# Routed tiles' tokens turned by transposing transfers instead of TensorE transposes

## The chip, the core and the metric

The kernel runs on one core of a Trainium2 chip. A core has TensorE (PE in the profile; its weight loads are PEld), VectorE (DVE), ScalarE (ACT), GpSimd (POOL) and SyncE (SP). They run their own instruction streams and wait for each other by semaphores. Sixteen DMA engines move data; in this kernel nearly all transfers are issued by SP, one after the other. The metric is the device time in microseconds (us) from start to end.

## What is computed

A decoder layer over 8 sequences of 256 tokens with 256 features each: causal self-attention with 16 heads, a cross attention with three gated recurrent updates, and a mixture-of-experts feed-forward part. Each of the three ends with a residual and a layer norm. All is float32. The change lies in the last part, of which the reference is, shortened:

```python
def _L0_ffn_ref(x, gate_w, gate_b, sh_w1, sh_b1, sh_w2, sh_b2, ew1, eb1, ew2, eb2):
    router_probs = softmax(einsum('bsd,de->bse', x, gate_w) + gate_b)
    expert_values, expert_indices = top_k(router_probs, k=2)
    expert_values = expert_values / (sum(expert_values, axis=-1, keepdims=True) + 1e-09)
    h = gelu(einsum('bsd,edi->bsei', x, ew1) + eb1)
    all_outputs = einsum('bsei,eid->bsed', h, ew2) + eb2
    moe_out = einsum('bse,bsed->bsd', weights_E, all_outputs)
    return x + _mlp(x, sh_w1, sh_b1, sh_w2, sh_b2) + moe_out
```

There are 8 experts, each an MLP 256 -> 1024 -> 256, of which each token uses its best two, and one shared MLP for every token.

## The kernel before

The 2048 tokens stand in four blocks of 512. Attention comes first (to about 340 us), then the recurrent part with the routing of finished blocks woven in (to about 640 us), then the experts.

**Routing by tables in DRAM.** For each token and each of its two experts the kernel computes a row number in a table `xd` in DRAM, in which each expert owns a stretch of rows, and GpSimd scatters the tokens there (`place`, L914). The tables `tei` and `tri` then tell, for every tile of work, which expert it belongs to and at which row it starts. A pair tile has 256 rows, a single tile 128. There are 21 tiles that always run, in the order pair, pair, single, five times, and then six pairs. Two more single tiles (`RARE`) stand under a condition and run only if a table says so.

**One tile.** Its parts, with the lines of the profile:

- `tile_fetch` (L1143, L1145): SP loads the row number from `tri` into a register and issues the transfer of the tokens, `xg`, tokens on partitions; 256 KB for a pair.
- `tile_weights` (L1157 to L1163): SP loads the expert's number from `tei` and issues the transfer of the first weight `w1` (1 MB; L1162) and its bias `bt`.
- `tile_turn` (L1178, L1180): TensorE transposes `xg` in blocks of 128x128 into PSUM, and VectorE copies the result to `xgT`, features on partitions.
- `tile_up` (L1075, L1084): `up`, in 16 float32 matmuls, each of which appears as two records in the profile, and the gelu on ScalarE.
- `tile_weights2` (L1169, L1170): transfer of the second weight `w2` (1 MB) and its bias `b2t`.
- `tile_down` (L1089, L618, L1193): the matmuls of the second layer, VectorE adds the bias into `yo`, and SP stores it into the table `yd`.

**Order.** For TensorE and ScalarE the order is that of the program text. For VectorE, GpSimd and SP a scheduler chooses the order in this stage, so it need not be that of the text; it moves register loads from `tei` and `tri` far ahead. In the text, step k of the loop over tiles is: up of k, fetch of k+3, first weight of k+2, turn of k+1, down of k-1, second weight of k+1. Both weights have two buffers: the w1 of tile k+2 waits for the up of tile k, the w2 of k+1 for the down of k-1. `xg` has four buffers, `xgT` two.

**Around it.** Before the first tile, four of the eight units of the shared MLP run (`shared_up`, `shared_down`); the other four come after the last tile, together with the gathering of the experts' rows by GpSimd (`fetch_back`, L1203), their sum on VectorE (`take_back`), the last layer norm and the store of the result (`finish`).

**A transfer that transposes** is already in the attention stage: `split` (L388, and L391 for half of the words of the last block on GpSimd) copies the float32 words of a matrix of 128x768 into two planes of 16-bit halves, SP issues one transposing transfer of the 128x1536 words (L394), and `joined` (L400) has VectorE put the halves of the turned planes together.

Of the kernel before, what the change touches and what calls it, by code (L numbers as in the profile page):

```python
# [10 lines left out]
F32 = mybir.dt.float32  # L11
I32 = mybir.dt.int32
U16 = mybir.dt.uint16
# [4 lines left out]
B, S, D = 8, 256, 256  # L18
# [3 lines left out]
NE, FF = 8, 1024  # L22
P = 128
DC = D // P
# [13 lines left out]
RT = 256  # L38
# [7 lines left out]
TILES = [t for k in range(NOFTEN) for t in (2 * k, 2 * k + 1, NPAIRT + k)]  # L46
# [19 lines left out]
def decoder_kernel(  # L66
# [23 lines left out]
    nc = tc.nc  # L90
# [6 lines left out]
    def big(name):  # L97
        return pools["big"].tile([P, 2, 512], F32, tag="big", name=name)

    def bank(name):  # L100
        return pools["bk"].tile([P, 512], F32, tag="bk", name=name)
# [13 lines left out]
    XT = [act.tile([P, DC, BLK], F32, tag=f"XT{i}", name=f"XT{i}") for i in range(NBLK)]  # L115
# [5 lines left out]
    ident = const.tile([P, P], F32, name="ident")  # L121
# [46 lines left out]
    b1c = vec_sb[:, 0 : (NE + 1) * FC].rearrange("p (e c) -> p e c", c=FC)  # L168
# [36 lines left out]
    def load_shared():  # L205
        w1_sb = sh.tile([P, DC, FF], F32, name="sh1")
        w2_sb = sh.tile([P, FC, D], F32, name="sh2")
        nc.sync.dma_start(w1_sb, sh_w1.rearrange("(c p) f -> p c f", p=P))
        nc.sync.dma_start(w2_sb, sh_w2.rearrange("(c p) d -> p c d", p=P))
        return w1_sb, w2_sb  # L210
# [56 lines left out]
    with (  # L267
# [234 lines left out]
        for k in range(last + 1):  # L502
            i, j = divmod(k, 2 * NPAIR)
# [38 lines left out]
    shared = load_shared()  # L542
# [60 lines left out]
    for h in range(2):  # L603
        n = (NSINGLE + 1 - h) // 2
# [458 lines left out]
    f2 = ctx.enter_context(tc.tile_pool(name="f2", bufs=2))  # L1063
    f1 = ctx.enter_context(tc.tile_pool(name="f1", bufs=1))
    wff = ctx.enter_context(tc.tile_pool(name="wff", bufs=2))

    def up(w1_sb, bias, rhs, name):
        hT = fh.tile([P, FC, RT], F32, tag="hT", name=f"hT_{name}")
        w = rhs.shape[2]
        for c2 in range(FC // 2):  # L1070
            ph = big(f"ph_{name}_{c2}")
            for a in range(2):
                c = 2 * c2 + a
                for dc in range(DC):
                    nc.tensor.matmul(  # L1075
                        ph[:, a, 0:w],
                        w1_sb[:, dc, ts(c, P)],
                        rhs[:, dc, :],
                        start=dc == 0,
                        stop=dc == DC - 1,  # L1080
                    )
            for a in range(2):
                c = 2 * c2 + a
                nc.scalar.activation(hT[:, c, 0:w], ph[:, a, 0:w], AF.Gelu_apprx_tanh, bias=bias[:, c : c + 1])  # L1084
        return hT
# [15 lines left out]
    HT = {}  # L1101

    def shared_up(u):
        i, h = divmod(u, BLK // RT)
        HT["s", u] = up(shared[0], b1c[:, NE, :], XT[i][:, :, ts(h, RT)], f"s{u}")

    def shared_bias(u):

# [24 lines left out]
    TI = {}  # L1133

    def groups(t):
        return 2 if t < NPAIRT else 1
# [4 lines left out]
    def tile_fetch(t):  # L1141

        row = nc.sync.value_load(tri[0:1, t : t + 1], min_val=0, max_val=ROWS - RT)  # L1143
        xg = f2.tile([P, 2, D], F32, tag="xg", name=f"xg_{t}", bufs=4)[:, 0 : groups(t), :]
        load = nc.sync.dma_start(xg, rows_of(xd, row, t))  # L1145
        for put in puts:
            tc.add_manual_dep(
                load.ins,
                put.ins.name,
                mybir.DependencyInfo(mybir.DependencyClass.Sync, mybir.DependencyReason.DATA),  # L1150
                reason="rows of the table",
            )
        TI[t] = [row, xg]

    def tile_weights(t):

        e = nc.sync.value_load(tei[0:1, t : t + 1], min_val=0, max_val=NE - 1)  # L1157
        w1_sb = wff.tile([P, DC, FF], F32, tag="w1", name=f"w1_{t}")
        w2_sb = wff.tile([P, FC, D], F32, tag="w2", name=f"w2_{t}")
        bt = f2.tile([P, FC], F32, tag="bt", name=f"bt_{t}", bufs=3)  # L1160
        b2t = f2.tile([P, D], F32, tag="b2t", name=f"b2t_{t}", bufs=3)
        nc.sync.dma_start(w1_sb, ew1[ds(e, 1), :, :].rearrange("e (c p) f -> p (e c) f", p=P))  # L1162
        nc.sync.dma_start(bt, vecs[:, ds(e * FC, FC)])  # L1163
        TI[t] += [w1_sb, w2_sb, bt, b2t, e]

    def tile_weights2(t):

        row, xgT, w1_sb, w2_sb, bt, b2t, e = TI[t]
        nc.sync.dma_start(w2_sb, ew2[ds(e, 1), :, :].rearrange("e (c p) d -> p (e c) d", p=P))  # L1169
        nc.sync.dma_start(b2t, b2[ds(e, 1), :].to_broadcast([P, D]))  # L1170

    def tile_turn(t):
        xg = TI[t][1]
        n = groups(t)
        pt = bank(f"xg_{t}")[:, 0 : DC * n * P].rearrange("p (c r) -> p c r", c=DC)
        for dc in range(DC):
            for k in range(n):
                nc.tensor.transpose(pt[:, dc, ts(k, P)], xg[:, k, ts(dc, P)], ident)  # L1178
        xgT = f2.tile([P, DC, RT], F32, tag="xgT", name=f"xgT_{t}")[:, :, 0 : n * P]
        nc.vector.tensor_copy(xgT, pt)  # L1180
        TI[t][1] = xgT

    def tile_up(t):
        row, xgT, w1_sb, w2_sb, bt, b2t, e = TI[t]
        HT["t", t] = up(w1_sb, bt, xgT, f"t{t}")

    def tile_down(t):
        row, xgT, w1_sb, w2_sb, bt, b2t, e = TI.pop(t)
        n = groups(t)
        po = down(w2_sb, HT.pop(("t", t)), f"t{t}", groups=n)  # L1190
        yo = f2.tile([P, 2, D], F32, tag="yo", name=f"yo_{t}")[:, 0:n, :]
        tt(yo, po[:, 0:n, :], b2t.unsqueeze(1).to_broadcast([P, n, D]), ALU.add)
        nc.sync.dma_start(rows_of(yd, row, t), yo)  # L1193
# [28 lines left out]

    nunit = NT // RT
    shared_up(0)
    place(1)
    residual(3)
# [5 lines left out]
    def parts(u):  # L1232
        next(part[u])
        next(part[u])
# [6 lines left out]
    route_rest(2)  # L1241
    route_rest(3)
    shared_up(1)
    place(2)
    next(part[1])
# [7 lines left out]
    for u in range(2, SHARED_FIRST):  # L1253
        shared_up(u)
        if u == SHARED_FIRST - 1:
            tile_fetch(TILES[2])
            tile_weights(TILES[1])
            tile_turn(TILES[0])
        parts(u)
    for u in range(SHARED_FIRST, nunit):  # L1260
        shared_bias(u)
    for k, t in enumerate(TILES):
        tile_up(t)
        for t2 in TILES[k + 3 : k + 4]:
            tile_fetch(t2)
        for t2 in TILES[k + 2 : k + 3]:
            tile_weights(t2)
        for t2 in TILES[k + 1 : k + 2]:
            tile_turn(t2)
        if k:  # L1270
            tile_down(TILES[k - 1])
        if k == NPAIRT:
            first_rare = nc.values_load(tei[0:1, NTILE : NTILE + 1], min_val=0, max_val=NE)
        for t2 in TILES[k + 1 : k + 2]:
            tile_weights2(t2)
# [3 lines left out]
    with tc.If(first_rare < NE):  # L1279
        for t in RARE:  # L1280
            tile_fetch(t)
            tile_weights(t)
            tile_weights2(t)
            tile_turn(t)
            tile_up(t)
            tile_down(t)
# [27 lines left out]
    for a in range(half):  # L1314
        n = half + a
# [69 lines left out]
```

## Time and profile before

Three runs took 1028.01, 1028.21 and 1026.47 us, with a median of 1028.01. The profile is of one execution.

| | |
|---|---|
| profiled execution, device time | 1024.5 us |
| its span, first to last instruction | 1022.8 us |
| granted TensorE clock, mean | 0.998 of full speed |
| VectorE, ScalarE, GpSimd busy | 485.0, 461.0 and 263.6 us |
| transfers of weights, 1024 KB each | 42, landing 5.7 us after issue (median) |
| transfers of `xg` of a pair, 256 KB | 16, landing 5.5 us after issue (median) |
| stores of `yo` of a pair, 256 KB | 16, landing 5.6 us after issue (median) |

The profile is a page of tables over one execution, and the trace behind it can be asked for single stretches. A group of instructions is told by its line in the kernel, its engine, its operation, and the tile written and the tiles read (`out<-in`), with the shape. Times are in us unless marked ns. A view of windows gives the busy time of each engine in a stretch, the granted clock, the share of the DMA engines' time that is in use and what they moved. The lengths of matmul records overlap, so the time that a piece of work holds TensorE is read from the starts.

### The profile page before, as it was taken

Reading aid. Unit: us, or ns where it says so; the run is one execution under the profiler, and the core shown is the slowest. Engines: PE = TensorE matmul, PEld = TensorE weight load, DVE = VectorE, ACT = ScalarE, POOL = GpSimd, SP = SyncE. Lnnn points to the kernel's source line nnn. Section 1 sums busy time; section 2 is a strip of 40 time slices with the busy share of each in tenths; the row PEclk is TensorE's granted clock in tenths of the full one; section 3 lists DMA queues with packets and bytes.
Section 4 is the critical chain, followed back from the end, with each engine's and each line's share of the span. In section 5 each row is a group of like instructions: output and inputs, shape, how many; then the busy total and the mean of one; then the engine's idle time right before and its main releaser. Section 6 shows DMA issues by size and latency. Waiting matters only on the chain. (4 is left out here: it accounts for less than half of the span.)

```text
span 1022.8 us, 13461 instructions
## 1 busy us (share of the span) xinstructions
PE 1009.1 (99%) x4586; PEld 697.2 (68%) x4586; DVE 485.0 (47%) x1378; ACT 461.0 (45%) x1140; POOL 263.6 (26%) x282
## 2 busy tenths in 40 slices
PE   9999999999999999999999999999999999999997
PEld 5444555555545855655665667888888888888886
DVE  4678776876898451444444568630100001010157
ACT  3577766766687023545545535322222222222232
POOL 2333433642488121212222003440000000000272
PEclk9999999999999999999999999999999999999999
DMA  9744443443567399970000001146766766754143
GB/s 324 138 79 88 84 77 63 78 78 62 79 110 128 114 348 348 349 260 0 1 0 1 1 0 42 54 142 197 253 208 218 260 212 226 238 170 148 48 124 100
DMA packets 191717, 139.26 MB, mean 136 GB/s; under 512 B 107103, under 2 KB 182687, under 8 KB 191647
## 3 DMA queue, kind: packets, MB, share of 16 engines
q1 hardware_dynamic: 187487, 127.89, 45.1%
q0 software_dynamic: 3072, 8.39, 2.6%
q10 hardware_dynamic: 1088, 2.10, 0.6%
q8 instruction: 37, 0.61, 0.2%
q14 instruction: 33, 0.27, 0.1%
HBM read 67.97 MB, written 45.22 MB: 111 GB/s over the span
## 5 line engine op out<-in xcount | busy, mean ns | idle before, releaser
L1084 ACT ACTIVATE hT_t<-ph_t,bt 128x256 f32<-128x256 f32 (+1 forms) x168 | 66.1, 444 | 193.0 <-issue 122.9
L357 ACT ACTIVATE sc<-sc,nmax 128x128 f32<-128x128 f32 (+1 forms) x256 | 113.2, 443 | 86.0 <-DVE nmax L344 85.5
L372 POOL TENSOR_TENSOR sc<-sc,sums 128x256 f32<-128x256 f32 (+1 forms) x128 | 105.3, 843 | 162.9 <-DVE sums L369 162.5
L761 PE MATMUL gate<-XT,whh_sb 128*128 128x512 f32 x288 | 133.8, 593 | 0.0
L1075 PE MATMUL ph_t<-xgT,w 128*128 128x256 f32 (+1 forms) x672 | 132.5, 355 | 0.8 <-ACT hT_t L1084 0.8
L1089 PE MATMUL pf_t<-w,hT_t 128*128 128x256 f32 x592 | 131.1, 379 | 0.0
L1075 PEld LDWEIGHTS ph_t<-xgT,w 128*128 128x128 f32 x672 | 116.2, 190 | 14.8 <-ACT hT_t L1084 1.0
L1089 PEld LDWEIGHTS pf_t<-w,hT_t 128*128 128x128 f32 x592 | 111.0, 190 | 14.3
L1203 POOL DMA_INDIRECT y<-yd,slot x32 | 30.7, 959 | 293.4 <-ACT hT_s L1084 283.9
L400 DVE COPY pT<-turned 128x1536 uint16<-128x1536 uint16 x64 | 89.7, 1401 | 1.3 <-DMA turned<-planes 1.3
L761 PEld LDWEIGHTS gate<-XT,whh_sb 128*128 128x128 f32 x288 | 54.3, 190 | 48.5 <-issue 46.2
L344 DVE CUSTOM_DVE_ANT_0 sc<-pp,mask 128x128 f32<-128x128 f32 (+1 forms) x256 | 75.8, 352 | 8.8 <-PE pp L332 8.2
L770 PEld LDWEIGHTS gate<-at,G 120*128 120x128 f32 x288 | 54.5, 189 | 29.9 <-issue 23.2
L388 ACT COPY planes<-sc 128x1536 uint16<-128x1536 uint16 x48 | 70.6, 1470 | 6.7 <-POOL sc L372 6.7
L770 PE MATMUL gate<-at,G 120*128 120x256 f32 x288 | 72.2, 379 | 0.4 <-DVE at L618 0.4
L1180 DVE COPY xgT<-xg 128x512 f32<-128x512 f32 (+1 forms) x21 | 13.2, 628 | 125.0 <-PE xg L1178 125.0
L618 DVE TENSOR_TENSOR yo<-pf_t,b2t 128x512 f32<-128x512 f32 (+1 forms) x21 | 13.2, 628 | 121.5 <-PE pf_t L1089 121.5
L307 PE MATMUL pq<-XT,wq_sb 128*128 128x512 f32 x128 | 63.4, 618 | 0.2 <-DVE XT L109 0.2
L307 PE MATMUL pq<-XT,wk_sb 128*128 128x512 f32 x128 | 63.2, 616 | 0.0
L317 PE MATMUL pv<-wv_sb,XT 128*128 128x512 f32 x128 | 59.7, 594 | 0.0
L414 PE MATMUL po<-pT,v 128*64 128x256 f32 (+1 forms) x512 | 55.7, 338 | 2.4 <-DVE pT L400 1.5
L430 PE MATMUL py<-wo_sb,ot 128*128 128x256 f32 x256 | 57.9, 381 | 0.0
(213 smaller groups left out, 1428.1 us busy)
## 6 DMA issues: line engine op xcount, KB each, us to landing
w<-in_ew_dram SPq DMA_DIRECT2D x42, 1024.0 KB, 5.7
xd<-zeros SPq DMA_DIRECT2D x1, 16640.0 KB, 51.3
yd<-zeros SPq DMA_DIRECT2D x1, 16640.0 KB, 99.4
xg<-xd SPq DMA_DIRECT2D x16, 256.0 KB, 5.5
yd<-yo SPq DMA_DIRECT2D x16, 256.0 KB, 5.6
b2t<-in_b_dram SPq DMA_DIRECT2D x21, 128.0 KB, 5.4
sh<-in_sh_w_dram SPq DMA_DIRECT2D x2, 1024.0 KB, 6.6
X<-in_x_dram SPq DMA_DIRECT2D x3, 512.0 KB, 11.5
```

The costliest lines, as they stand in the source:

```text
L307: nc.tensor.matmul(pq, w[:, dc, ts(pr, P)], XT[i][:, dc, :], start=dc == 0, stop=dc == DC - 1)
L317: nc.tensor.matmul(pv, XT[i][:, dc, ts(n, P)], wv_sb[:, dc, ts(hf, 512)], start=dc == 0, stop=dc == DC - 1)
L344: nc.vector.tensor_tensor_reduce(out=sc[:, h, seg[t]], in0=pp[h][:, seg[t]], in1=mask[:, seg[t]], scale=-(HD**-0.5), scalar=3.0e38, op0=AL ...
L357: nc.scalar.activation(sc[:, h, seg[t]], sc[:, h, seg[t]], AF.Exp, scale=-1.0, bias=nmax[:, t, h : h + 1], accum_out=sums[:, t, h : h + 1],)
L372: nc.gpsimd.tensor_tensor(sc[:, :, seg[t]], sc[:, :, seg[t]], sums[:, t, :].unsqueeze(2).to_broadcast([P, 2, w]), ALU.mult,)
L388: nc.scalar.copy(planes, words)
L400: nc.vector.tensor_copy(pT.rearrange("p h c -> p (h c)").bitcast(U16).rearrange("p (n w) -> p w n", w=2), turned.rearrange("p (w c) q -> p ...
L761: nc.tensor.matmul(pg[:, oc, :], whh_sb[:, dc, o], XT[i][:, dc, :], start=dc == 0, stop=not given and dc == DC - 1,)
L770: nc.tensor.matmul(pg[:, oc, ts(bi, S)], G[:, BPB * i + bi, o], AT_[p][:, bi, :], start=not hidden, stop=not hidden or bi == BPB - 1,)
L1075: nc.tensor.matmul(ph[:, a, 0:w], w1_sb[:, dc, ts(c, P)], rhs[:, dc, :], start=dc == 0, stop=dc == DC - 1,)
L1084: nc.scalar.activation(hT[:, c, 0:w], ph[:, a, 0:w], AF.Gelu_apprx_tanh, bias=bias[:, c : c + 1])
L1089: nc.tensor.matmul(po, hT[:, c, ts(a, P)], w2_sb[:, c, :], start=c == 0, stop=c == FC - 1)
```

## The change

The tokens of every tile but the first are no longer transposed by TensorE. `tile_split(t)` has GpSimd copy the tile's `xg` into two planes of 16-bit halves (`xp`), and SP issues one transposing transfer of them into `xt`; a pair has 128x1024 such words, a single 128x512. `tile_turn(t)` now only has VectorE join the halves into `xgT`. In the text the split of tile k+2 follows its first weight in step k. The first tile keeps the transposes, in `tile_turn_first`. `xgT` is laid out anew: group of 128 tokens, then half of the features, then token, so `up` reads its right operand for a pair as two runs of 128 words instead of one run of 256. Buffers `xp` and `xt` have two copies each.

```diff
-    def up(w1_sb, bias, rhs, name):
+    def up(w1_sb, bias, rhs, name, width=RT):
+
         hT = fh.tile([P, FC, RT], F32, tag="hT", name=f"hT_{name}")
-        w = rhs.shape[2]
+        w = width
...
-                        rhs[:, dc, :],
+                        rhs(dc),
...
-        HT["s", u] = up(shared[0], b1c[:, NE, :], XT[i][:, :, ts(h, RT)], f"s{u}")
+        HT["s", u] = up(shared[0], b1c[:, NE, :], lambda dc: XT[i][:, dc, ts(h, RT)], f"s{u}")
...
+    def tile_split(t):
+
+        xg = TI[t][1]
+        n = groups(t) * D
+        planes = f2.tile([P, 4 * D], U16, tag="xp", name=f"xp_{t}")[:, 0 : 2 * n].rearrange("p (w n) -> p w n", w=2)
+        nc.gpsimd.tensor_copy(planes, xg.rearrange("p k d -> p (k d)").bitcast(U16).rearrange("p (n w) -> p w n", w=2))
+        turned = f2.tile([P, 2 * 2 * D // P, P], U16, tag="xt", name=f"xt_{t}")[:, 0 : 2 * n // P, :]
+        nc.sync.dma_start_transpose(turned, planes.rearrange("p w n -> p (w n)"))
+        TI[t][1] = turned
+
     def tile_turn(t):
+        turned = TI[t][1]
+        n = groups(t)
+        xgT = f2.tile([P, 2, DC, P], F32, tag="xgT", name=f"xgT_{t}")[:, 0:n, :, :]
+        nc.vector.tensor_copy(
+            xgT.rearrange("p k c q -> p (k c q)").bitcast(U16).rearrange("p (n w) -> p w n", w=2),
+            turned.rearrange("p (w c) q -> p w (c q)", w=2),
+        )
+        TI[t][1] = xgT
+
+    def tile_turn_first(t):
+
         xg = TI[t][1]
-        n = groups(t)
-        pt = bank(f"xg_{t}")[:, 0 : DC * n * P].rearrange("p (c r) -> p c r", c=DC)
-        for dc in range(DC):
-            for k in range(n):
-                nc.tensor.transpose(pt[:, dc, ts(k, P)], xg[:, k, ts(dc, P)], ident)
-        xgT = f2.tile([P, DC, RT], F32, tag="xgT", name=f"xgT_{t}")[:, :, 0 : n * P]
+        xgT = f2.tile([P, 2, DC, P], F32, tag="xgT", name=f"xgT_{t}")[:, 0 : groups(t), :, :]
+        pt = bank(f"xg_{t}")[:, 0 : DC * groups(t) * P].rearrange("p (k c q) -> p k c q", c=DC, q=P)
+        for k in range(groups(t)):
+            for dc in range(DC):
+                nc.tensor.transpose(pt[:, k, dc, :], xg[:, k, ts(dc, P)], ident)
         nc.vector.tensor_copy(xgT, pt)
         TI[t][1] = xgT
 
     def tile_up(t):
         row, xgT, w1_sb, w2_sb, bt, b2t, e = TI[t]
-        HT["t", t] = up(w1_sb, bt, xgT, f"t{t}")
+        HT["t", t] = up(w1_sb, bt, lambda dc: xgT[:, :, dc, :], f"t{t}", groups(t) * P)
...
-            tile_turn(TILES[0])
+            tile_turn_first(TILES[0])
+            tile_split(TILES[1])
...
             tile_weights(t2)
+            tile_split(t2)
...
             tile_weights2(t)
+            tile_split(t)
             tile_turn(t)
```

## The prediction

> **What bounds the kernel now.** First the page's busy table and the granted clock, then the tile stage alone (690 to 961 us in this trace), by engine, in order of time.
>
> ```profile
> PE 1009.1 (99%) x4586; PEld 697.2 (68%) x4586; DVE 485.0 (47%) x1378; ACT 461.0 (45%) x1140; POOL 263.6 (26%) x282
> PEclk9999999999999999999999999999999999999999
> ```
>
> TensorE is busy for 99% of the span at full clock, so work taken from it shortens the run unless something else is late in its place. The timeline of TensorE in the tile stage (start, length, engine, line, operation, count) shows the work that goes:
>
> ```profile
> 721.29 0.60 PE L1178 MATMUL xg<-ident,xg 128*128 128x128 f32 x4
> 721.72 7.07 PE L1089 MATMUL pf_t<-w,hT_t 128*128 128x256 f32 x32
> 728.63 7.07 PE L1075 MATMUL ph_t<-xgT,w 128*128 128x256 f32 x32
> 735.54 0.60 PE L1178 MATMUL xg<-ident,xg 128*128 128x128 f32 x4
> 735.98 3.62 PE L1089 MATMUL pf_t<-w,hT_t 128*128 128x256 f32 x16
> 739.43 7.07 PE L1075 MATMUL ph_t<-xgT,w 128*128 128x256 f32 x32
> 746.34 0.38 PE L1178 MATMUL xg<-ident,xg 128*128 128x128 f32 x2
> 746.56 7.07 PE L1089 MATMUL pf_t<-w,hT_t 128*128 128x256 f32 x32
> ```
>
> Starts count here, since lengths overlap: a pair's four transposes hold TensorE 0.44 us (735.54 to 735.98), a single's two 0.22, an up or a down of a pair 6.91, a single's up 3.70 and down 3.45. I number the 21 tiles 0 to 20 in their order; 2, 5, 8, 11 and 14 are singles.
>
> **What goes.** Fifteen pairs and five singles lose their transposes: 15 x 0.44 + 5 x 0.22 = 7.7 us. Tile 1 saves more: its up follows its transposes directly and waited for the copy.
>
> ```profile
> 702.04 0.60 PE L1178 MATMUL xg<-ident,xg 128*128 128x128 f32 x4
> 703.47 7.14 PE L1075 MATMUL ph_t<-xgT,w 128*128 128x256 f32 x32 [0.83 <-ACT hT_t L1084]
> ```
>
> From 702.48 (four transposes end) to 703.47 are 1.0 us; the copy of VectorE that the up needs ran 702.68 to 703.37, so the releaser named here is not the one that held it. Together 8.7 us of TensorE time, all on the path. The two rare tiles change likewise but aren't run (L1143 has 21 loads, not 23).
>
> A rule speaks against this. The Trainium skill ("VectorE: DVE Perf Modes", The three transpose paths, and Rules for kernel authors) says to transpose 128x128 on TensorE where PSUM will do, and prices a 16-bit block at 390 ns there and 1309 ns as a DMA. By it the gain would be 70 x 0.39 = 27 us, and a pair (8 blocks of 16 bits) would hold the DMAs 10.5 us beside the 9.8 they have already (below), 20 us against a 13.8 us tile: some 90 us slower. Both its prices are of one block alone; this trace has 0.11 us per TensorE block in a row, and the attention stage has the same transfer as the new one:
>
> ```profile
> L394 SPq DMA_TRANSPOSE turned<-planes x54: 1414/1433/2564, 62.8 to 319.8; - x54
> DMA to landing us min/median/max: 3.6/3.6/5.3
> 180.00:240.00 60.00, 59.47 (x309) 32.03 (x309) 46.70 (x154) 40.72 (x119) 29.89 (x32) 1.00 0.44 77
> 712.00:718.00 6.00, 6.00 (x31) 5.33 (x30) 0.22 (x1) 0.00 (x0) 0.00 (x0) 1.00 1.00 336
> ```
>
> (Its issues on SP as min/median/max ns, landing, and two windows whose last columns are clock, DMA share and GB/s.) One transfer of 12 blocks each 4.85 us, nearly alone, keeps the DMAs busy for 0.44: 2.1 us for 12, so 1.4 for a pair (8) and 0.7 for a single (4). I take the row.
>
> **What is added, by engine.**
> DMA: the share is 0.63 to 0.78 in the 30 us windows of this stage, about 0.71, so a triple of two pairs and a single (36.0 us now) uses 25.6; with 3.5 more in 34.9 us it is 0.83. No saturation on average; bursts reach 1.00 already (712 to 718).
> GpSimd: 20 splits on an engine idle from 680.6 to 964.6. The copy of 128x768 16-bit words at L391 takes 1.46 us, so 1.95 for a pair, 1.0 for a single. Only later splits queue behind it.
> VectorE: the L1180 copy (0.69 and 0.42) becomes a copy of words; L400 takes 1.40 for 1536, so 0.93 and 0.47. VectorE is busy about 3 us in 30. Tile m+3's copy stands ahead of tile m's yo there; it needs up m+1 and its transfer, both done before down m ends.
> TensorE: `up` reads its right operand as two runs of 128 instead of 256 in a row. No row has this form. Below: 0. Above: 10% on the pairs' 512 records at 0.216 us, 11 us. I take 0, as a single's operand is one run either way.
>
> **The SP queue** is where the price lies. SP issues every transfer in order, and the new one waits for its split, which waits for xg; behind it stand weights. In the settled stage this costs nothing: w1 of tile k+2 is asked for when up k ends and used two downs and one up later (14 us or more; landing is 5.7), and w2 of k+1 has 17 us between request and use. But at the start SP is the bottleneck:
>
> ```profile
> 690.28 0.57 SPq L1163 DMA_DIRECT2D bt<-in_vecs_dram  x1
> 691.63 0.38 SPq L1145 DMA_DIRECT2D xg<-xd  x1
> 706.46 0.38 SPq L1162 DMA_DIRECT2D w<-in_ew_dram  x1
> ```
>
> Between the last two, SP loads 25 table entries into registers: 14.8 us, 0.59 each. In the changed program's order of SP, transfers 1, 2 and 3 stand inside this stretch, 20 of the loads remain ahead of the w1 of tile 2, and the others move behind, before later weights. Step by step: transfer 1 at 690.85 (its xg landed at 686.6), taking 1.4; a load; xg 3 at about 693.5; transfer 2 waits for xg 2 (688.59 + 6.5 landing + 1.0 split = 696.1); three loads; transfer 3 waits for xg 3 (693.5 + 6.6 + 1.95 = 702) and ends at 703.2; 16 loads (9.5) put w1 of tile 2 at 712.7 instead of 706.46. It landed in 4.9 then, so 717.6. TensorE, now ahead, wants it at 695.13 + 3 x 6.91 = 715.86: **a stall of 1.7**.
> Going on with the landings measured there (6 to 7.7 after a request under load): w2 of tile 1 at 713.8, lands 720.9, wanted at 721.3; xg 4 at 715, transfer 4 done on SP by 726, three loads, w2 of tile 2 at 728.3, lands 734.3, wanted 735.1; xg 5 at 730.2, transfer 5 waits until 737.7, four loads, w2 of tile 3 at 741.2, lands 747.2, wanted at 745.5: **1.7 more**. After that the slack grows (w1 of tile 6 lands at 759.5, wanted at 764.7) and the loads run out.
>
> The length of a transfer's issue is the uncertain term: 1.43 us for 12 blocks, so 0.95 to 1.43 for 8. Behind a 1 MB weight, as most will be, there is one row, and one far longer behind the whole opening backlog:
>
> ```profile
> 329.15 0.41 SPq L208 DMA_DIRECT2D sh<-in_sh_w_dram  x1
> 329.66 2.06 SPq L394 DMA_TRANSPOSE turned<-planes  x1
> L394 SPq DMA_TRANSPOSE turned<-planes x64: 1414/1434/10835, 22.0 to 329.7; - x64
> ```
>
> I take 1.0 to 1.4, and 2.06 as the bad end. Some five transfers stand ahead of a late weight; at 2.06 each the stalls become about 5.
>
> **Sum.** 8.7 - 1.7 - 1.7 = 5.3 us gained. The profiled execution took 1024.5 us (span 1022.8): 1019.2. It lies 3.5 us below the median of the runs, 1028.0, which I lower by the same 5.3: **1022.7 us**. What follows the last tile (up of unit 4 at 961) only moves earlier: its gathers wait for the last yd, issued as before.
>
> **Rivals.**
> 1. Full gain: SP's delay is hidden, because loads are shorter between waits or the first weights land in less. 8.7 us, 1019.3. For it: two stalls of 1.7 are small against the roughness of my times. Against: both come from delays of 6 us or more on SP with slack that I could count.
> 2. The stalls eat it: issues of 2.5 to 3.5 us, stalls of 7 to 11: within 2 us of 1028. For it the 2.06 row, and bursts at share 1.00.
> 3. **Slower**, by one mechanism: a transfer's issue blocks SP until what is queued ahead has drained, as in the 10.8 us row, where some 11 us of loads lay ahead. Place: transfers 1 to 5, behind weights. A w1 with bt and xg ahead is 4 to 5 us, so 3.8 over my 1.2 for each of about four: 15 more, stalls 18, net 9.7 slower, 1037.7. It decides from an issue of about 3.5 us. Against it: at 329.66 a whole weight lay ahead (landing 5.7 to 7.6) and the issue took 2.06.
> 4. The two-run operand slows the pairs' ups: 11 - 5 = 6 slower, 1034. Nothing in the trace speaks for it.
>
> **How the numbers follow.** What a measurement can tell from no change here is 0.2%, 2 us. Forecast (gain of 2 to 7) 0.42, full gain 0.13, eaten up 0.15, slower by SP's queue 0.24, by the operand 0.06. So faster 0.55, same 0.15, slower 0.30. The range runs from 1018.5 to 1034: it leaves out the far half of rival 3 and a little below rival 1. The likeliest case alone: 1020.5 to 1026.
>
> **What will show it.** The L1178 rows of TensorE shrink to tile 0's four. Right: the timeline has one gap of TensorE before tile 2's up and one before tile 3's down, 1 to 3 us each, none after about 760 us; SP issues w1 of tile 2 at about 713; up records stay at 379 ns; the DMA share of 720 to 930 is 0.8 to 0.85. Wrong: transfer issues of 3 us or more, gaps all through the stage (then the DMAs or the order of SP are the bound), or longer up records.

## The result and the profile after

The change makes the kernel faster by about half a per cent. Six runs of each on the same chip: 1020.44 us after (1019.09 to 1021.81) and 1026.47 before (1026.26 to 1028.21), a ratio of 0.9943 with an interval of 0.993 to 0.9957. That is 5.9 us, against a forecast of 5.3.

From the page after, the busy table and the DMA row, and below them the DMA row of the page before:

```profile
PE 1003.7 (98%) x4516; PEld 691.0 (68%) x4516; DVE 485.8 (48%) x1378; ACT 461.3 (45%) x1140; POOL 282.7 (28%) x302
DMA  9744433443566399980000001125899988964143
```

```profile
DMA  9744443443567399970000001146766766754143
```

TensorE has 70 matmul records fewer and is still the bound, at a granted clock of 0.996 on average. What is new is the DMA row: in the slices of the tile stage (the 29th to the 35th) the DMAs are at 8 to 9 tenths, where they were at 6 to 7.

The same stretch of TensorE's timeline as before (start, length, engine, line, operation, count, and in brackets the idle time ahead of it and who ended it):

```profile
696.90 13.98 PE L1076 MATMUL ph_t<-xgT,w 128*128 128x256 f32 x64
710.71 7.07 PE L1090 MATMUL pf_t<-w,hT_t 128*128 128x256 f32 x32
718.75 3.95 PE L1076 MATMUL ph_t<-xgT,w 128*128 128x128 f32 x32 [0.97 <-DMA w<-in_ew_dram]
...
739.90 7.07 PE L1076 MATMUL ph_t<-xgT,w 128*128 128x256 f32 x32
747.47 7.14 PE L1090 MATMUL pf_t<-w,hT_t 128*128 128x256 f32 x32 [0.50 <-DMA w<-in_ew_dram]
755.45 3.95 PE L1076 MATMUL ph_t<-xgT,w 128*128 128x128 f32 x32 [0.83 <-DMA w<-in_ew_dram]
...
957.15 14.05 PE L1076 MATMUL ph_s<-XT,sh 128*128 128x256 f32 x64
```

The ups of tiles 0 and 1 now run as one block of 64 records, with no transposes and no wait for a copy between them. Three waits stand in their place, each for a weight: tile 2's up starts at 718.75 instead of 710.71 + 6.91 = 717.62 (1.13), tile 3's down at 747.47 instead of 739.90 + 6.91 = 746.81 (0.66), tile 5's up at 755.45 instead of 754.38 (1.07). After 756 us there is none.

A ruler for what follows is **the stage**: from the first matmul of tile 0's up to that of unit 4's up. Before it ran from 695.13 to 961.02, 265.89 us (the line of its end is below); after from 696.90 to 957.15, 260.25: 5.64 less.

```profile
961.02 14.05 PE L1075 MATMUL ph_s<-XT,sh 128*128 128x256 f32 x64
```

The profiled executions themselves differ by only 3.4 us (1024.5 and 1021.1), because the one after lost 1.77 us ahead of the stage. The window of 650 to 660 us shows it, first before, then after:

```profile
650.00:660.00 10.00, 10.00 (x59) 9.12 (x59) 6.42 (x57) 5.01 (x11) 0.20 (x1) 1.00 0.04 14
```

```profile
650.00:660.00 10.00, 10.00 (x50) 8.73 (x50) 6.06 (x54) 4.14 (x9) 0.28 (x1) 0.83 0.04 14
```

The granted clock (third number from the right) was 0.83 there, for 1.00 before. This slump stands in some traces and not in others, so the stage is the better ruler for a microsecond.

SP's queue at the start of the stage after:

```profile
691.61 0.67 SPq L1164 DMA_DIRECT2D bt<-in_vecs_dram  x1
692.39 4.21 SPq L1180 DMA_TRANSPOSE xt<-xp  x1
697.40 0.41 SPq L1146 DMA_DIRECT2D xg<-xd  x1
698.53 5.59 SPq L1180 DMA_TRANSPOSE xt<-xp  x2
713.72 0.41 SPq L1163 DMA_DIRECT2D w<-in_ew_dram  x1
```

The transfers and the register loads between 692 and 714 put the w1 of tile 2 at 713.72, 16.8 us after the stage's start; before it was 11.3 (706.46). The new operations themselves, by line, on GpSimd, SP and VectorE:

```profile
L1178 POOL COPY xp<-xg x20: 615/1042/1172, 688.4 to 902.3; 128x1024 uint16<-128x1024 uint16 x15, 128x512 uint16<-128x512 uint16 x5
L1180 SPq DMA_TRANSPOSE xt<-xp x20: 1190/1246/4212, 692.4 to 903.5; - x20
L1187 DVE COPY xgT<-xt x20: 458/747/753, 700.9 to 915.6; 128x1024 uint16<-128x1024 uint16 x15, 128x512 uint16<-128x512 uint16 x5
```

(Minimum, median and maximum in ns.)

### The profile page after: what moved, and what is told of

It reads as the page before. It is cut to its first block, busy times and chain, and to the rows that moved or that the text cites. A ratio compares the mean times of both kernels' runs of the same rounds, so it can differ in the third digit from the quotient of the medians.

```text
span 1019.2 us, 13377 instructions
## 1 busy us (share of the span) xinstructions
PE 1003.7 (98%) x4516; PEld 691.0 (68%) x4516; DVE 485.8 (48%) x1378; ACT 461.3 (45%) x1140; POOL 282.7 (28%) x302
## 5 line engine op out<-in xcount | busy, mean ns | idle before, releaser
L1187 DVE COPY xgT<-xt 128x1024 uint16<-128x1024 uint16 (+1 forms) x20 | 13.5, 676 | 151.9 <-DMA xt<-xp 106.6
L1178 POOL COPY xp<-xg 128x1024 uint16<-128x1024 uint16 (+1 forms) x20 | 18.8, 942 | 202.1 <-DMA xg<-xd 202.1
L1076 PE MATMUL ph_s<-XT,sh 128*128 128x256 f32 x256 | 58.6, 388 | 0.2
```

The costliest lines, as they stand in the source:

```text
L1076: nc.tensor.matmul(ph[:, a, 0:w], w1_sb[:, dc, ts(c, P)], rhs(dc), start=dc == 0, stop=dc == DC - 1,)
```

## The experiments

Theory: 8.7 us of TensorE time go, and about 3 come back because SP, in order, issues a few early weights late. Rivals: the DMAs' bandwidth causes the waits (B), or the gain on TensorE is less than the starts say (A). Stage and time of all:

| kernel | stage, us | less than before | ratio of times (interval) |
|---|---|---|---|
| after | 260.25 | 5.64 | 0.9943 (0.993 to 0.9957) |
| after_again | 260.62 | 5.27 | 0.9946 (0.9929 to 0.9964) |
| e1_no_turn | 257.14 | 8.75 | 0.993 (0.9915 to 0.9944) |
| e2_both | 267.56 | -1.67 | 1.0025 (1.0013 to 1.0037) |
| e3_act_queue | 261.16 | 4.73 | 0.9966 (0.9952 to 0.9979) |
| e4_first4 | 259.30 | 6.59 | 0.9939 (0.9925 to 0.9952) |
| e5_twice | 267.26 | -1.37 | 1.0028 (1.0014 to 1.0042) |
| e6_w1_three | 259.91 | 5.98 | 0.9926 (0.9911 to 0.9941) |
| e7_act_from2 | 258.65 | 7.24 | 0.9934 (0.9917 to 0.9952) |
| e8_two_ahead | 257.14 | 8.75 | 0.9936 (0.9917 to 0.9956) |

All diffs are against the changed kernel.

**e1_no_turn: the removed part alone.**

```diff
     def tile_split(t):
-        ...
+        pass
     def tile_turn(t):
-        ...
+        nc.vector.tensor_copy(xgT, xg.rearrange("p k (c q) -> p k c q", c=DC))
```

> This kernel leaves out the turning of every tile but the first: VectorE copies xg into xgT as it is, so the experts multiply unturned tokens. Ruler for all runs: from the first matmul record of tile 0's up to that of unit 4's up, 265.9 us before and 260.3 after. My theory (8.7 us of TensorE time go, and 2.9 come back as waits for weights that SP issues late): with neither transposes nor transfers the stage takes 265.9 - 8.7 = 257.2, no wait for a weight, w1 of tile 2 issued some 12 us after tile 0's up starts as before, time about 8.7 less than before (ratio 0.9915). Rival A (TensorE gains less than the starts say, the rest is in how stages follow each other): 259 or more.

First and last line of the stage in its timeline of TensorE, and the DMAs from 730 to 930 us:

```profile
696.74 8.58 PE L1076 MATMUL ph_t<-xgT,w 128*128 128x256 f32 x39
953.88 14.05 PE L1076 MATMUL ph_s<-XT,sh 128*128 128x256 f32 x64
730.00:930.00 200.00, 200.00 (x987) 177.60 (x986) 16.04 (x32) 53.57 (x136) 0.00 (x0) 1.00 0.67 221
```

257.14: the 8.7 are right to 0.05, and rival A falls. Nothing waits for a weight, and SP issues the w1 of tile 2 at 707.39, 10.65 us after the stage's start. What the transfers give back in the change is 260.25 - 257.14 = 3.1 us.

**e2_both: the added part alone.** The transposes stay, the transfers are made besides.

```diff
-        TI[t][1] = turned
...
     def tile_turn(t):
-        ...
+        tile_turn_first(t)
```

> The transposes stay on TensorE for every tile, and the splits and transposing transfers are made besides, unread. My theory (the added part costs only waits for late weights at the start): TensorE's tiles are longer by what the transposes take and so want tile 2's w1 1.7 us later, after which the late w1 just about arrives; stage 265.9 to 267, time as before within 1.5 us. Rival B (the DMAs are the bound, share 0.99 after at 750 to 780): the same transfers cost 3 us or more here too, and the waits go on past the first six tiles.

The stage is 1.67 us longer than before, beyond the expected 1.1, and the time is 1.9 us longer, where 1.5 was the most expected. The wait at tile 2's up is gone, as expected; three short ones stand at tile 4's up, tile 3's down and tile 5's up (idle records of 0.29, 0.28 and 0.39), none later. Counted from start to start they are 1.6 us of the 1.67. So the added part costs 1.7 us where TensorE is slower, and 3.1 where it is faster and asks sooner. Rival B's 3 us or more and its later waits are not seen.

**e3_act_queue: nothing behind the transfers on SP.**

```diff
-        nc.sync.dma_start_transpose(turned, ...)
+        nc.scalar.dma_start_transpose(turned, ...)
```

> The change as it is, but the transposing transfers are issued from ScalarE's queue, so nothing stands behind them on SP. My theory (order of SP): w1 of tile 2 is issued some 12 us after tile 0's up starts instead of 17, no wait for weights over 0.3 us, stage 257.2 to 258, about 2.5 us less than after. Rival B (bandwidth): the same bytes move, so 2 to 3 us of waits stay, stage 260. Rival C (a transfer's issue of 1.2 to 4 us delays the gelu behind it on ScalarE): waits of up's matmuls for hT appear, 2 us or more.

SP issues the w1 of tile 2 at 706.37, 11.1 us after the stage's start (695.27), and no matmul waits for a weight. Yet the stage is longer than after. Its timeline of TensorE, the landing of transfer 1, and two windows:

```profile
704.43 8.83 PE L1076 MATMUL ph_t<-xgT,w 128*128 128x256 f32 x32 [2.09 <-DVE xgT L1187]
DMA to landing us min/median/max: 15.3/15.3/15.3
704.40:707.00 2.60, 2.57 (x8) 2.12 (x9) 1.22 (x2) 0.00 (x0) 0.91 (x1) 0.63 0.00 0
730.00:930.00 200.00, 200.00 (x988) 177.59 (x987) 19.98 (x34) 53.56 (x136) 14.68 (x15) 1.00 0.94 243
```

One wait none of the theories named: transfer 1, issued by ScalarE at 688.3 amid three weights from SP (685.35, 686.46 and 689.39), landed 15.3 us later, so tile 1's up began 2.25 us late (695.27 + 6.91 = 702.18), and its 32 records took 8.83 us instead of 7.07 at a clock of 0.63. 2.25 + 1.76 = 4.0, which is all that separates it from 257.14. Against rival B, that the DMAs' load makes the weights late, it is decisive: the DMA share rose to 0.94, above the 0.85 of after, and no weight was late. For the weights, what matters is when they are asked for; tile 1's tokens met a backlog on the DMAs (the w1 of 689.39 took 14.0 us too), whose cause stays open. Rival C (a gelu delayed) is not seen.

**e4_first4: no transfer inside the stretch of register loads.** (`FIRST_TURNED` is 4.)

```diff
-            tile_split(TILES[1])
...
-            tile_split(t2)
+            if k + 2 >= FIRST_TURNED:
+                tile_split(t2)
...
-            tile_turn(t2)
+            (tile_turn if k + 1 >= FIRST_TURNED else tile_turn_first)(t2)
```

> Tiles 0 to 3 are turned by TensorE, tiles 4 to 20 by transfers. My theory: the three transfers inside SP's stretch of register loads cause the wait at tile 2, so it goes; the waits at tile 3's down and tile 5's up stay in part. Given up: 1.44 at tile 1, 0.22 at tile 2, 0.44 at tile 3, 2.1 together; won back 1.1 to 2.9: stage 259.4 to 261.3, time as after within 1.5 us. Rival B (bandwidth): the waits at 747 and 755 stay whole or grow, stage 261.3 or more.

259.30. All three waits are gone, also those at tiles 3 and 5, which stand behind transfers that this kernel still makes: the delay of the first three transfers was carried through SP's queue to the sixth tile. Tile 5's w1 shows it: here SP issues it 43.2 us after the stage's start (741.67), after the change 50.0 (746.86). It lands no faster, in 9.3 us for 8.4, and yet is in time.

**e5_twice: the added load doubled.**

```diff
+        again = f2.tile([P, 2 * 2 * D // P, P], U16, tag="xt2", ...)
+        nc.sync.dma_start_transpose(again, planes.rearrange("p w n -> p (w n)"))
```

> Every transposing transfer is issued twice on SP, the second into a buffer that nobody reads. Measured so far: the DMA share of 730 to 930 us is 0.67 with no transfers and 0.85 with them, on SP's queue. Rival B (bandwidth is next to bind): a second set adds 0.18 and more, past 1.00, so TensorE waits for weights all through the stage: stage 264 to 275. My theory for the change itself (only the start was short, the settled stage had slack of 8 us and more per weight): the second issue of 1.2 us for each adds to the waits of the first six tiles, 2 to 4 us, and the settled tiles stay without waits: stage 262 to 264.

267.26: my number missed, rival B's range holds it. The second issue took 2.26 us (median), not the expected 1.2. Its longer waits:

```profile
718.99 5.33 PE L1076 MATMUL ph_t<-xgT,w 128*128 128x128 f32 x32 [3.16 <-DMA w<-in_ew_dram]
...
778.18 7.14 PE L1076 MATMUL ph_t<-xgT,w 128*128 128x256 f32 x32 [1.26 <-DMA w<-in_ew_dram]
786.81 7.14 PE L1090 MATMUL pf_t<-w,hT_t 128*128 128x256 f32 x32 [1.48 <-DMA w<-in_ew_dram]
815.87 7.14 PE L1076 MATMUL ph_t<-xgT,w 128*128 128x256 f32 x32 [0.94 <-DMA w<-in_ew_dram]
```

They reach tile 10 (816 us), past the start, and then all but cease (0.15 at 893), although the DMA share is 0.96 to 0.98 from 840 on. The first of them also brought a slow clock, 1.5 us more (last section). So neither account is whole: the start is worse than I had it, the settled tiles have less slack than the 8 us I gave them, and a share of 0.97 alone doesn't stall TensorE.

**e6_w1_three: an earlier w1.**

```diff
-        w1_sb = wff.tile([P, DC, FF], F32, tag="w1", name=f"w1_{t}")
+        w1_sb = wff.tile([P, DC, FF], F32, tag="w1", name=f"w1_{t}", bufs=3)
```

> The change with three buffers for w1 instead of two: tile 2's w1 no longer waits for tile 0's up, and SP's order has it right after tile 3's xg, ahead of transfers 2 and 3 and of all but a few register loads. My theory: the wait at tile 2's up goes (1.1 us); 18 loads now stand ahead of tile 2's w2, and waits at a down may stay: stage 257.2 to 259.2, 1 to 3 us less than after. Rival B (bandwidth): 260 or more, the waits only change their place.

259.91, a miss by 0.7 to the theory's range and within a hair of rival B's 260. The wait at tile 2 is gone, as expected (w1 asked for at 696.76). One wait is left, at tile 7's up:

```profile
755.98 1.27 SPq L1180 DMA_TRANSPOSE xt<-xp  x1
...
765.29 0.38 SPq L1163 DMA_DIRECT2D w<-in_ew_dram  x1
...
774.24 7.14 PE L1076 MATMUL ph_t<-xgT,w 128*128 128x256 f32 x32 [2.48 <-DMA w<-in_ew_dram]
```

Tile 7's w1 is the one issued at 765.29. It waits for no buffer now, but in SP's order it stands behind a transfer that was held for its split until 755.98 and eight register loads. SP's order again, in another place. But the DMAs have a part in it: it landed 8.8 us after its issue, where the median of a weight before was 5.7, which would have been in time for 771.54, when TensorE was free. The mean share of 0.78 from 730 to 930 hides this; from 766 to 771 it was 1.01. So the run doesn't settle between SP's order and bandwidth by itself.

**e7_act_from2 and e8_two_ahead: a version without waits.** e7 is e3 with tile 1 turned by TensorE; e8 also puts tile 1's transposes right behind tile 0's. The diff is e8's, without the line that it shares with e3:

```diff
-            tile_split(TILES[1])
+            tile_turn_first(TILES[1])
...
         for t2 in TILES[k + 1 : k + 2]:
-            tile_turn(t2)
+            if k:
+                tile_turn(t2)
```

> Tile 1 is turned by TensorE, tiles 2 to 20 by transfers from ScalarE's queue. The transfers of e3_act_queue left one wait, for tile 1's tokens, and none for weights. My theory: with tile 1 on TensorE nothing waits; 8.7 less the 1.44 of tile 1 remain: stage 258.6, no slump of the clock after a gap. Rival: the queue of ScalarE is slow under load (landing 7.0 median there, 15.3 at most), so another tile's tokens come late: 260 or more.

> As e7_act_from2, but tile 1's four transposes stand right behind tile 0's, ahead of the shared unit's down, so its copy on VectorE is long done when its up starts. My theory: the wait of 1.0 us at tile 1's up goes and its 0.44 us of transposes fall ahead of the ruler, so the stage is 258.65 - 1.43 = 257.2 with no wait; of the whole time 8.3 us are gained on before, ratio 0.992. Rival (tile 2's or a later tile's tokens come late from ScalarE's queue): 259 or more.

e7 came to 258.65 and e8 to 257.14 (697.48 to 954.62), both as expected, with no wait for a weight or for a transfer; e7 keeps the 1.0 us at tile 1's up, e8 has no wait at all. By the stage e8 takes 3.1 us less than the change; 0.44 of it has only moved ahead of the stage. The whole times don't tell them apart: 0.9934 and 0.9936 have intervals that overlap that of the change, and e8's gain on before was 6.9 us, for 8.3 expected.

**after_again.**

> The change as it is, once more beside e8_two_ahead on the same chip. My theory: stage 260.3 with the same three waits for weights, at tile 2's up, tile 3's down and tile 5's up, 2.9 us together, ratio 0.994. If the waits come from the DMAs' chance rather than from the fixed order of SP, they should stand elsewhere or differ by more than 1 us.

```profile
719.26 3.95 PE L1076 MATMUL ph_t<-xgT,w 128*128 128x128 f32 x32 [1.72 <-DMA w<-in_ew_dram]
747.86 7.15 PE L1090 MATMUL pf_t<-w,hT_t 128*128 128x256 f32 x32 [0.19 <-DMA w<-in_ew_dram]
755.17 3.95 PE L1076 MATMUL ph_t<-xgT,w 128*128 128x128 f32 x32 [0.16 <-DMA w<-in_ew_dram]
```

The same three places; the first wait is longer (1.9 us) and the others shorter, as they would be where a tile that starts late gives the next weights time. Together they are as long within 0.4: the stage is 260.62.

## Why the prediction was right

- **What goes.** 8.7 us forecast, 8.75 measured by e1. Reading starts instead of record lengths, and counting the 1.0 us at tile 1 that the trace put down to the wrong releaser, both held.
- **The rule against the change.** By an estimate from the prices of the Trainium skill ("VectorE: DVE Perf Modes", The three transpose paths) for one block it would have been some 90 us slower; the row of the attention stage was the right guide for the sign. But the row was too small: 112 blocks in 16 transfers between 730 and 930 us should have cost 20 us of DMA time, and raised the share from 0.67 (e1) to 0.85, which is 36. In e4, with the same 16 transfers, it was 0.81, 28 us. A row taken from a stage with little else on the DMAs doesn't price the transfer beside weights. Why it costs more there was not tried. That the forecast share of 0.83 is still near the measured 0.85 is luck: the share without the transfers was taken as 25.6 of 34.9, 0.73, and is 0.67. The mean share didn't decide the time.
- **GpSimd and VectorE.** 1.95 and 0.93 us forecast for a pair; 1.05 and 0.75 measured. The L391 row that I scaled ranged from 0.82 to 1.52 us; its low end scales to 1.10. The mean of a row from a busy stage was the wrong choice, and made the waits for splits too long by 0.9.
- **The two-run operand.** Taken as free, and free: the pairs' up records have 379 ns before and after.
- **SP's queue.** The w1 of tile 2 was forecast at 712.7 in the time of the trace before; it was 713.72 in a trace whose stage began 1.77 later, so 0.75 early. The stalls forecast at tile 2's up and tile 3's down are there, 1.13 and 0.66 for 1.7 each. The second is below the 1 to 3 us that was forecast for each. A third, of 1.07 at tile 5's up, was not foreseen: the prediction lets the slack grow after tile 3's down and works out no time for this w1. Its buffer was free from 736.45, but SP issued it at 746.86, behind transfer 5 and tile 3's w2, and it landed 8.4 us later, beside a store and tile 4's w2. In sum 2.9 us of waits for 3.4, and that this is so near is in part luck: the two that were forecast come to 1.8.
- **The length of a transfer's issue.** 1.24 us is the median, within the 1.0 to 1.4 taken, but seven of the twenty took over 1.8. Issues of 3 us or more, named as a sign against the forecast, came three times: 4.21 at transfer 1, 4.15 at transfer 6, each with two weights still in flight, and 3.08 at transfer 9. So rival 3's long issues exist, but not its about four in a row at the start. The first fell where SP had to wait for splits anyway; the second stood ahead of a w1 that still landed 1.2 us before its use.
- **The base.** The 1022.7 stood on a median of 1028.0; with six runs that median is 1026.47. This, not the gain, is most of the distance to 1020.44.

## What to carry to other kernels

On an engine that is the bound, work that can go elsewhere is worth its start-to-start time; but then price the queue through which its replacement is issued, item by item: here 8.75 us went and 3.1 came back because SP issued weights late. The higher mean share of the DMAs didn't stall TensorE, but a weight that was asked for late, among others, also landed late (8.4 and 8.8 us). A row for a new operation should be taken with its spread, and from a stage as loaded as the one it goes to. And look for a start-up stretch in which the issuing engine has work of its own, since a delay there is carried on for several tiles.

## What was not expected of the hardware

- After e3's gap of 2.25 us in TensorE's work the granted clock was 0.63 for 4.6 us, which cost 1.76 us more; e5's gap of 3.2 us was followed by a single's up of 5.33 us instead of 3.87. But e6's idle time of 2.48 us, longer than the 2.09 of e3, was not followed by it (clock 1.00, 7.14 us for the 32 records), nor were the shorter gaps of the other runs. So the length of the gap alone doesn't decide; what does stays open. The Trainium skill ("TensorE: Matmul & The Clock Gate", Why this matters for your kernels) warns of gaps over about 3 us; here 2.25 from start to start was enough once.
- A slump of about the same 1.7 us comes without a gap, at 652 us, at the end of 32 matmuls of 128x8: in the traces of after, after_again, e1 and e8, twice as long in e4 (clock 0.66 from 650 to 660), and not in those of before, e2, e3, e5, e6 and e7. It may be what sets the executions of one kernel apart: the 51 of before that were taken beside the experiments fall into three groups, 1024.2 to 1024.7, 1026.0 to 1026.7 and 1027.8 to 1028.2 us, with mean clocks of 0.998, 0.996 to 0.997 and 0.995. Executions with none, one and two slumps would make such steps; only profiled executions could show where the clock fell. The profile of before, at 1024.5, has none, which would be why it lay 3.5 us under the first median.
- The same transfers issued from ScalarE's queue landed later (7.0 us in e3, 6.5 in e7, 6.3 in e8, median) than from SP's (4.7 after, 4.1 in after_again). The DMA share was higher in e3 and e7 (0.94 and 0.91, for 0.85), but not in e8 (0.86). The cause stays open.
